# A two-layer graph network on one core: the whole program's instruction queues ordered by another model of durations

## The chip, the cores and the metric

One core of a Trainium2 chip. The metric is the device time of one execution in microseconds (us). The core has five engines with a queue of instructions each: TensorE (PE in the profile, with PEld for its weight loads), VectorE (DVE), ScalarE (ACT), GpSimd (POOL) and SyncE (SP), which here only starts transfers. A queue is fixed when the program is built.

## The reference

64 graphs of 256 nodes with 256 features each, in float32. Two layers, each followed by a residual sum and a layer norm.

```python
# layer 0, of one graph: adj and x are 256x256
deg = adj.sum(-1); deg = where(deg != 0, deg, 1); r = deg ** -0.5
h = (r[:, None] * adj * r[None, :] + max(alpha, 1e-10) * I) @ x
x = layernorm(x + h @ W.T + b)
# layer 1
xc = x.T
h = relu(bn1(conv1d(xc, conv1, width 1)))
x_conv = relu(bn2(conv1d(h, conv2, width 17, pad 8)) + xc).T
s = x @ w_se.T + b_se                      # 3 columns
A = exp(-squared_distance(s, s))           # 256x256
x_nmp = A @ relu(x @ w_msg.T + b_msg)
gi = concat(x_conv, x_nmp) @ w_ih.T + b_ih; gh = x @ w_hh.T + b_hh
r = sigmoid(gi_r + gh_r); z = sigmoid(gi_z + gh_z)
n = tanh(gi_n + r * gh_n)
x = layernorm(x + (1 - z) * n + z * x)
```

## The kernel before

Line numbers are those of the profile before.

**Rounds.** The 64 graphs go in four rounds of 16 (`Q = 16`, `NQ = 4`). The convolution of width 17 is done in the frequency domain: each graph gives 8 pieces of 32 nodes, so a round fills the 128 rows of a matmul with 16 x 8 pieces. A round has three stages.

1. *Graphs* (`graphs`, L879). For each graph `layer0` (L329) and `layer1` (L403) are generators that are stepped in turn. Layer 0: transposes of the adjacency (`p_adjT`, L361), a copy on ScalarE (L362), `p_hT` (L382), its copy (L387), `p_out` (L392), a sum on VectorE (L396), a layer norm. Layer 1: transposes of the result (`p_x1T`, L411) and their copy to `xn` (L412), the first convolution (`p_conv`, L420), its bias on VectorE (`h`, L423) and relu on ScalarE (L424), messages (`p_msg`, L441), the DFT (`p_dft`, L455) and its copy, transposed distance rows (`p_rows`, L468; `dist_l` L470 and `dist_r` L472), `p_dist` (L479), the exponential (L480) and mask (L481), and the sum over neighbours (`p_nmp`, L486).
2. *Products* (`products`, L528). In 12 steps the spectra are multiplied by the kernel's spectra `u`, which are streamed from memory (`p_k`, L510). `VM` is overwritten in place, and an inverse FFT (`real_transform`, `complex_begin`, `complex_end`) runs over it on VectorE, hundreds of operations of 0.4 to 0.7 us at L559 to L688. It ends with stores to `xc_d`.
3. *Gates* (`gru`, L766). For each graph: transposes of the convolution's result (`p_xcT`, L750), sums of inputs on GpSimd (`sums`, L761 to L764), seven blocks of `p_rz` (L780), their sums on VectorE (`first`, L793 and on), tanh on ScalarE, `p_n` (L817), `gn` (L822 to L826), a layer norm and the store. Each gate unit fills six PSUM tiles (four `p_rz`, two `p_n`), which take the four banks of the pool `psacc` in turn.

The stages of neighbouring rounds overlap: four gate units of a round run beside the next round's graphs, and the other twelve beside the next round's products. In round 0 there is other work beside the graphs: the 13 *weight sets* (`weights`, L274 to L296) that make `u`. A set loads 4 rows of taps, scales them (L279), does eight matmuls (`p_u`, L287), copies them to `u_set` (L290), forms a difference on VectorE (L292) and a sum on GpSimd (L293), and writes three arrays to `ud` (L295). `PLACES` (L877) says at which piece of a graph a piece of the other work is taken:

```python
PLACES = (("other",), ("layer0",), (), (), ("layer0",), ("other", "layer0"), ())
```

**What sets the order.** The generators set the order in which instructions are recorded, and with it their priority. Then a planner goes through the recorded program: it keeps a clock for each engine, advances it by a model of how long each instruction takes, and puts into each engine's queue, at each moment of that clock, the ready instruction of the highest priority. So a queue's order depends on the recorded order and on the modelled durations; an instruction that the model finds ready early can be queued ahead of others that were recorded before it. The chip keeps the queue's order whatever the real durations are. In three places an order is written by hand, with `tc.issue_after` (L219, L346, L372), all of them at the start.

**Buffers that bind.** PSUM: `ps` and `psacc` with four banks each. `taps`: 2. `u_set`: 2 for each of its four kinds. `xn`: 2. `sums`, `trz`, `nn`, `h`, `hT`, `msg`, `aT`: 1.

Of the kernel before, what the change touches and what calls it, by code (L numbers as in the profile page):

```python
# [26 lines left out]
def kernel(  # L27
# [39 lines left out]
    NQ = B // Q  # L67
    assert N == 256 and D == 256 and B % Q == 0 and TAPS == FL - NT + 1 and FL == 3 * NT // 2

    const = ctx.enter_context(tc.tile_pool(name="const", bufs=1))  # L70
    dram = ctx.enter_context(tc.tile_pool(name="dram", bufs=1, space=bass.MemoryType.DRAM))

# [986 lines left out]
```

## Time and profile before

| | us |
|---|---|
| device time, median of two runs | 2188.94 (2186.56 to 2191.32) |
| span of the profiled execution | 2186.0 |
| TensorE busy | 2067.5 (95%) |
| VectorE busy | 1547.1 (71%) |
| ScalarE busy | 831.2 (38%) |
| GpSimd busy | 664.5 (30%) |
| bytes moved | 305.64 MB, mean 140 GB/s |
| mean granted TensorE clock | 0.985 |

A float32 matmul stands in the profile as two records, so 4 matmuls are "x8". A record's own duration is longer than the distance to the next, since matmuls are pipelined: four matmuls of 256 columns start 1.73 us after the four before them. In a list of instructions the bracket says how long the engine sat idle before them and who released it. In the list of waits the numbers are the total, the number of times, and the longest. In time, the graphs of round 0 go to about 289 us; the products `p_k` of the four rounds lie at 289 to 393, 641 to 752, 1161 to 1271 and 1682 to 1790 us; what remains of a round's gates follows its products, then come the next round's graphs; after 1790 only gates are left.

### The profile page before, as it was taken

The numbers are of one execution on the slowest core, as the hardware profiler recorded it, in microseconds if no ns is written. First come the engines' busy times: TensorE is split into PE (matmuls) and PEld (weight loads), VectorE is DVE, ScalarE is ACT, GpSimd is POOL, SyncE is SP. The second block draws the span as 40 slices with busy tenths as digits, with TensorE's granted clock in tenths as the row PEclk, the third lists the DMA queues.
The fourth block names the chain that finished last, engine by engine and source line by source line (L and its number), as shares of the span: only waits on it lengthen the run. The fifth ranks groups of instructions, "written<-read, shape, count | busy, mean of one in ns | idle before, by whom it ended". The sixth has DMA issues, their size and how long they took to land.

```text
span 2186.0 us, 28897 instructions
## 1 busy us (share of the span) xinstructions
PE 2067.5 (95%) x9805; PEld 1750.7 (80%) x9805; DVE 1547.1 (71%) x3691; ACT 831.2 (38%) x1847; POOL 664.5 (30%) x640
## 2 busy tenths in 40 slices
PE   6999899969999988999999998899999999899998
PEld 5888778758888876888888887788888887778887
DVE  5555458875568799655557889855565879987766
ACT  3665533445531123455452122446543112222222
POOL 2445310122322233223231224322231223344442
PEclk9999999989999999999999999999999999999999
DMA  3765656443346644434336654433334654344441
GB/s 110 239 193 194 222 178 207 151 134 102 111 137 201 191 130 108 131 91 123 105 101 190 207 144 130 116 114 108 102 97 126 205 160 118 114 121 111 105 113 53
DMA packets 251331, 305.64 MB, mean 140 GB/s; under 512 B 18324, under 2 KB 229864, under 8 KB 251184
## 3 DMA queue, kind: packets, MB, share of 16 engines
q1 hardware_dynamic: 183680, 200.46, 30.0%
q10 hardware_dynamic: 44480, 67.39, 8.7%
q0 software_dynamic: 23024, 35.95, 8.2%
q8 instruction: 78, 1.28, 0.2%
q14 instruction: 69, 0.57, 0.1%
HBM read 200.62 MB, written 103.06 MB: 139 GB/s over the span
## 4 chain that ended last, share of the span: by engine, by line
PE 50%; DVE 14%; issue 6%; POOL 6%; ACT 4%; DMA 0%; ACTq 0%; POOLq 0%; SPq 0%; DVEq 0%
PE p_rz L780 18%; PE p_n L817 9%; PE p_k L510 8%; PE p_nmp L486 2%; PE p_out L392 2%; PE p_dft L455 2%; PE p_conv L420 2%; POOL sums L762 2%; PE p_hT L382 1%; PE p_msg L441 1%; POOL ln_rs L308 1%; POOL sums L764 1%; PE p_dist L479 1%; POOL sums L763 1%; DVE gn L822 1%
## 5 line engine op out<-in xcount | busy, mean ns | idle before, releaser
L780 PE MATMUL p_rz<-wrz,sums 128*128 128x256 f32 x1536 | 355.8, 383 | 19.4 <-DVE gn L822 9.8
L817 PE MATMUL p_n<-wn,inputs 128*128 128x256 f32 x1536 | 353.0, 383 | 16.2 <-DVE first L793 15.7
L780 PEld LDWEIGHTS p_rz<-wrz,sums 128*128 128x128 f32 x1536 | 288.4, 191 | 70.7 <-issue 15.8
L817 PEld LDWEIGHTS p_n<-wn,inputs 128*128 128x128 f32 x1536 | 286.6, 191 | 62.6 <-DVE first L793 19.0
L780 PE MATMUL p_rz<-wrz,inputs 128*128 128x256 f32 x1152 | 272.9, 380 | 2.4 <-ACT inputs L752 1.8
L308 POOL TENSOR_TENSOR ln_rs<-ln_rs,neg_half 128x2 f32<-128x2 f32 x129 | 100.2, 777 | 537.3 <-DVE ln_rs L307 451.5
L780 PEld LDWEIGHTS p_rz<-wrz,inputs 128*128 128x128 f32 x1152 | 216.7, 190 | 33.9 <-ACT inputs L752 3.8
L352 POOL TENSOR_TENSOR dis<-deg,neg_half 128x2 f32<-128x2 f32 x64 | 48.6, 760 | 425.1 <-DVE deg L350 320.4
L829 ACT ACTIVATE nn<-gn 128x256 f32<-128x256 f32 x128 | 53.2, 416 | 326.0 <-DVE gn L826 325.5
L510 PE MATMUL p_k<-u,VM 128*128 128x256 f32 x736 | 175.1, 380 | 0.0
L318 ACT ACTIVATE x_g<-x_g,ln_mr,ln_rs 128x256 f32<-128x256 f32 x128 | 70.0, 593 | 256.4 <-DVE ln_mr L316 256.4
L510 PEld LDWEIGHTS p_k<-u,VM 128*128 128x128 f32 x736 | 138.6, 190 | 19.6 <-DMA u<-ud 0.7
L455 PE MATMUL p_dft<-fwd,h 128*128 128x240 f32 x512 | 121.4, 382 | 24.2 <-ACT h L424 23.1
L761 POOL TENSOR_TENSOR sums<-inputs 128x384 f32<-128x384 f32 x64 | 69.6, 1087 | 230.2 <-issue 172.3
L420 PE MATMUL p_conv<-wc,xn 128*128 128x259 f32 x512 | 127.4, 391 | 12.1 <-ACT xn L412 12.1
L455 PEld LDWEIGHTS p_dft<-fwd,h 128*128 128x128 f32 x512 | 98.2, 196 | 41.2 <-ACT h L424 32.9
L382 PE MATMUL p_hT<-adjT,x 128*128 128x256 f32 x512 | 126.8, 392 | 2.2 <-ACT adjT L362 1.5
L486 PE MATMUL p_nmp<-aT,msg 128*128 128x256 f32 x512 | 123.6, 385 | 2.6 <-DVE aT L481 2.6
L375 POOL TENSOR_TENSOR x_t<-x_t,b_t 128x512 f32<-128x512 f32 x64 | 84.8, 1325 | 134.5 <-ACT x L374 94.0
L392 PE MATMUL p_out<-w,hT 128*128 128x256 f32 x512 | 122.8, 382 | 1.1 <-ACT hT L387 0.9
L441 PE MATMUL p_msg<-wmsg,xn 128*128 128x256 f32 x512 | 122.1, 381 | 0.0
L420 PEld LDWEIGHTS p_conv<-wc,xn 128*128 128x128 f32 x512 | 96.8, 192 | 31.5 <-ACT xn L412 17.3
(154 smaller groups left out, 3838.6 us busy)
## 6 DMA issues: line engine op xcount, KB each, us to landing
u<-ud SPq DMA_DIRECT2D x284, 256.0 KB
xn_d<-xn ACTq DMA_DIRECT2D x64, 512.0 KB
inputs<-xn_d SPq DMA_DIRECT2D x64, 512.0 KB
ud<-u_set POOLq DMA_DIRECT2D x39, 480.0 KB, 6.1
adj_t<-in_adj_dram SPq DMA_DIRECT2D x64, 256.0 KB
x_t<-in_x_dram SPq DMA_DIRECT2D x64, 256.0 KB
x_d<-x ACTq DMA_DIRECT2D x64, 256.0 KB
x_g<-x_d SPq DMA_DIRECT2D x64, 256.0 KB
```

The costliest lines, as they stand in the source:

```text
L308: nc.gpsimd.tensor_tensor(rs[:, : len(chunks)], rs[:, : len(chunks)], neg_half[:, : len(chunks)], op=ALU.pow)
L318: nc.scalar.activation(y[:, c, :], y[:, c, :], AF.Identity, bias=mr[:, c : c + 1], scale=rs[:, c : c + 1])
L375: nc.gpsimd.tensor_tensor(x_t, x_t, b0_t.unsqueeze(1).to_broadcast([P, NCH, D]), op=ALU.add)
L382: nc.tensor.matmul(p[:, k, :], x1[:, mc, k * P : (k + 1) * P], adjT[:, mc, 1 - mc : 3 - mc, :].rearrange("p n q -> p (n q)"), start=mc == ...
L392: nc.tensor.matmul(p[:, c, :], hT[:, k, c * P : (c + 1) * P], w0[:, k, :], start=k == 0, stop=k == DCH - 1)
L420: nc.tensor.matmul(p, x1T[:, k, c * P : (c + 1) * P], wc1[:, k, :], start=k == 0, stop=k == DCH - 1)
L441: nc.tensor.matmul(p[:, c, :], x1T[:, k, c * P : (c + 1) * P], wmsg[:, k, :], start=k == 0, stop=k == DCH - 1)
L455: nc.tensor.matmul(p[:, t0 * FL : t1 * FL], h[:, c, k * P : (k + 1) * P], fwd[:, first : first + t1 - t0, :].rearrange("p t f -> p (t f)") ...
L486: nc.tensor.matmul(p[:, k, :], msg[:, mc, k * P : (k + 1) * P], aT[:, mc].rearrange("p n q -> p (n q)"), start=mc == 0, stop=mc == NCH - 1,)
L510: nc.tensor.matmul(p[:, j * D : (j + 1) * D], v[:, k, :], u[:, k, :], start=k == 0, stop=k == DCH - 1)
L780: nc.tensor.matmul(p[:, j * D : (j + 1) * D], a[:, k], wrz[:, b, k], start=k == 0, stop=k == HALF - 1)
L817: nc.tensor.matmul(p[:, o * D : (o + 1) * D], lhsT, w, start=j == 0, stop=j == len(part) - 1)
```

## The change

One statement is added at the head of the kernel's function. It opens a block, held open to the end of the function, with an option that is off by default:

```diff
     assert N == 256 and D == 256 and B % Q == 0 and TAPS == FL - NT + 1 and FL == 3 * NT // 2
 
+
+    ctx.enter_context(tc.block(schedule_with_timeline_sim=True))
     const = ctx.enter_context(tc.tile_pool(name="const", bufs=1))
```

For all that is recorded in the block the planner keeps its clocks by the other model of durations it has, a timeline simulation of the instructions, in place of its usual one. The purpose is queues that fit durations nearer to the chip's. No operation, operand, buffer or transfer is added, removed or resized: all five engines get the same instructions, in another order. Line numbers after the change are two higher.

The two orders, built from the two sources, differ from the start on. Three excerpts of TensorE's queue, before and after, give the manner; the names are those of the tiles written, the numbers are matmuls:

```
graphs 0 and 1 of round 0, before: p_conv 4, p_u 4, p_adjT 4, p_msg 4, p_dft 4, p_rows 2, p_hT 4, p_dist 2, p_u 4, p_out 4, p_nmp 4, p_x1T 4, p_conv 1, p_u 4, p_conv 3
graphs 0 and 1 of round 0, after:  p_u 8, p_x1T 4, p_u 8, p_conv 4, p_adjT 4, p_msg 4, p_u 8, p_dft 4, p_rows 2, p_hT 4, p_u 8, p_dist 2, p_out 4, p_u 8, p_nmp 4, p_x1T 4, p_u 8, p_conv 4
graphs 5 to 15 of round 0, before: as above, p_u 8 in each up to graph 12
graphs 5 to 15 of round 0, after:  p_conv 4, p_adjT 4, p_msg 4, p_dft 4, p_rows 2, p_hT 4, p_dist 2, p_out 4, p_nmp 4, p_x1T 4
graphs beside gates, before: p_conv 4, p_adjT 4, p_msg 4, p_dft 4, p_rows 2, p_hT 4, p_dist 2, p_rz 6, p_xcT 4, p_out 4, p_nmp 4, p_x1T 4, p_n 6, p_conv 4
graphs beside gates, after:  p_conv 4, p_adjT 4, p_msg 4, p_rz 6, p_n 3, p_dft 4, p_rows 2, p_hT 4, p_n 8, p_dist 2, p_n 1, p_out 4, p_rz 7, p_nmp 4, p_x1T 4, p_conv 4
```

On VectorE the operations of the inverse FFT move against those of graphs and gates, and on GpSimd the sums and the writes of `ud` move against the layer norms.

## The prediction

> **What bounds the kernel now.** I read the page's first two parts, then the chain, then who TensorE waits for, then the worst stretch in order of time.
>
> ```profile
> PE 2067.5 (95%) x9805; PEld 1750.7 (80%) x9805; DVE 1547.1 (71%) x3691; ACT 831.2 (38%) x1847; POOL 664.5 (30%) x640
> PE   6999899969999988999999998899999999899998
> PE 50%; DVE 14%; issue 6%; POOL 6%; ACT 4%; DMA 0%; ACTq 0%; POOLq 0%; SPq 0%; DVEq 0%
> ```
>
> TensorE is busy in 95% of the span, so an order can win at most what it idles: 2186.0 - 2067.5 = 118.5 us, plus what a lowered clock stretched. The second row shows where: the start, slice 8 (the end of round 0) and small dips. The waits of TensorE itself (first rows of that view):
>
> ```profile
> PE p_dft L455 <- ACT h L424: 23.1, 9, 9.6
> PE p_n L817 <- DVE first L793: 15.7, 13, 2.4
> PE p_conv L420 <- ACT xn L412: 12.1, 11, 3.9
> PE p_rz L780 <- DVE gn L822: 9.8, 9, 1.6
> PE p_rz L780 <- POOL sums L762: 9.3, 8, 2.5
> PE p_dist L479 <- DVE dist_r L472: 7.5, 7, 1.4
> ```
>
> Each is a round trip through another engine with too little matmul work queued in between. The timeline of PE at the worst place shows two kinds:
>
> ```profile
> 447.87 2.02 PE L420 MATMUL p_conv<-wc,xn 128*128 128x259 f32 x8 [0.73 <-ACT xn L412]
> 449.73 0.60 PE L361 MATMUL p_adjT<-ident,adj_t 128*128 128x128 f32 x4
> 450.16 1.89 PE L441 MATMUL p_msg<-wmsg,xn 128*128 128x256 f32 x8
> 461.61 3.57 PE L455 MATMUL p_dft<-fwd,h 128*128 128x240 f32 x8 [9.56 <-ACT h L424]
> 470.44 0.69 PE L468 MATMUL p_rows<-ident,scols 128*128 128x128 f32 x2 [5.25 <-DVE scols L433]
> ```
>
> First, a convolution right behind the transposes p_x1T that feed it costs 0.73 us. Second, VectorE had FFT work queued ahead of h, and the DFT waited 9.56 us. The busy time by stretches gives the clock and the transfer rate:
>
> ```profile
> 60.00:90.00 30.00, 29.89 (x149) 24.82 (x149) 18.38 (x41) 17.08 (x40) 14.19 (x13) 1.00 0.79 248
> 452.00:475.00 23.00, 8.10 (x22) 5.59 (x22) 19.55 (x58) 7.19 (x11) 1.97 (x2) 0.63 0.40 133
> 1820.00:1960.00 140.00, 122.91 (x560) 101.88 (x559) 129.45 (x265) 32.31 (x66) 54.11 (x49) 1.00 0.42 118
> ```
>
> (Columns: stretch, length; busy PE, PEld, DVE, ACT, POOL; granted clock; DMA share; GB/s.) In the last stretch VectorE, 129.45 of 140 us, is the limit, not TensorE.
>
> **What the Trainium skill says.** "PSUM — Partial Sum Buffer", section Engine vs sequencer instructions: the queues of ScalarE, VectorE and GpSimd are strict FIFO, and matmuls start in program order. The trace agrees: the matmuls behind the DFT at 461.61 did not overtake it. So the queue order alone decides what a wait holds up. "TensorE: Matmul & The Clock Gate", section HAM oscillation, warns of idle gaps over some 3.4 us, after which the array runs at half clock. It agrees: behind the 9.56 us gap eight passes took 3.57 us instead of 1.89, at a mean clock of 0.63. "DMA: Bandwidth & Descriptors", section Specifications, gives about 358 GB/s of HBM per core. No stretch here reaches it; the busiest moved 248 at a share of 0.79, from which I estimate a ceiling of 248/0.79 = 314.
>
> **The change, part by part.** No instruction is added or removed: both programs have the same matmuls and vector instructions; only queue positions differ. I compared the two orders engine by engine and priced the work between marks with start-to-start times of the trace before (a 256-column matmul 0.43 us, a 128x512 VectorE operation 0.60, a 128x256 one 0.34). Line numbers are those before.
>
> 1. *Convolution behind its transposes (L411, L420).* A convolution waits for the copy of p_x1T for 0.73 us less the matmul time queued between. Before, 9 of 64 graphs have less than that: 6.0 us in sum. After, 39 have, 34 of them nothing at all: 25.6 us. TensorE is the bound there and nothing hides it: **+19.6 us**.
> 2. *The other round trips.* The same count for rows to dist (0.92 us needed), dist to nmp (1.7) and hT to out (0.9) gives 0.9, 3.3 and 0.3 us before, 3.7, 5.1 and 0.9 after: **+5 us**. Between convolution and DFT neither order has less than 1.7 us, which the trace shows to be enough when VectorE is free.
> 3. *The weight sets (L287 to L295).* Before, eight p_u matmuls sit in each of 13 graphs, spread over 203 us of TensorE work. After, there are four sets to a graph and all 13 within 81 us (graph to graph 26.4, 26.4, 23.0 us of TensorE work, then twelve graphs of about 12.6 with none). VectorE (52 us of work in that stretch) and GpSimd (64 us) fit. Transfers do not: 39 writes of ud x 0.49 MB = 19.2 MB, taps 4.2, gate weights 2.4, and x, adj, xn and x1 of three to four graphs 4.7, sum 30.5 MB; without the last two sets' writes, which may land later, 27.6 MB. At my 314 GB/s that is 88 us, at the observed 248 it is 111. Each u_set has two buffers, held from the copy (3.5 us for eight matmuls) over sums (3.0) and issue (1.2) to landing (6.1 median): 14 us for two sets, or 7 us each, against 26.4/4 = 6.6 us of TensorE work. So the stall is 7 to 30 us; I take **+20 us**, and 0 to 45 for the range. What waits behind it: the copy on ScalarE for a free u_set holds the copies of the graph queued behind, and then TensorE.
> 4. *Start.* After, the first p_u stand before p_x1T of graph 0, and dft_w before ln_mr on VectorE. Before, TensorE did p_x1T and two convolutions (2.2 us) before it waited for dft_w until 36.26; after, it sits idle from about 28 to 36, over the clock gate's limit. 2.2 us plus some 4 us of slow clock: **+6 us**.
> 5. *VectorE at the end of round 0.* Before, the stretch between two graphs' h (L423) that overloads VectorE is one of 23.0 us of its work against 12.6 us of TensorE's, and in all 12 us more than TensorE has. After, three in a row, 20.7, 22.2 and 15.8 against 12.6: 21 us more. **+9 us**.
> 6. *VectorE at the tails of rounds 1 to 3.* From one gate unit (gru) to the next, marked by first (L793): before, 13.6 to 17.1 us of VectorE against 14.8 to 16.6 of TensorE in the worst units, overload 2 to 3 us a round. After, units of 21.5 and 19.8 against 14.8 and 14.3 in rounds 1 and 2, and 20.2, 20.1, 18.4 against 14.8 in round 3: overload 12, 12 and 14 us. But the totals over the tail are equal (round 3: 127 and 128 us), and at parity before already lost some 17 us in 1820 to 1960. What is paid in a lump after is then not paid in small change. I take **+4 us a round, +12**; the bounds are 0 and 32.
> 7. *An early GpSimd sum.* Before, sums (L761) stood ahead of ln_rs at 265 us and waited for its input's transfer; TensorE lost 5.1, 0.9 and 1.7 us and ran at half clock (0.64 from 265 to 284). Worth about 14 us in all. After, a sum is again placed ahead of layer norms, among graphs 5 to 6, but transfers are lighter there. I take half: **-7 us**.
>
> Scalar copies, loads of adj and x, stores: nothing, since they lie beside TensorE. Sum: 19.6 + 5 + 20 + 6 + 9 + 12 - 7 = 65 us. 2188.9 + 65 = **2254 us**.
>
> **Rivals.**
> *A, nearly no change.* The transfers keep up, since the first bits of a set can run ahead, and the tails even out: parts 1, 2 and half of 4 stay and the 14 us of part 7 come back: 20 + 5 + 3 - 14 = +14, 2203 us. For it: in the stretch 60 to 90 the DMA share was only 0.79. Against: 27.6 MB in 81 us would need 341 GB/s.
> *B, faster.* The new order dissolves the waits at 452, 787 to 865, 1306 to 1385 and 1820 to 1960 (about 22, 14, 15 and 17 us, with some 18 us of slow clock) and the sum at 265 (14), at the price of part 1 and 2 alone: 25 - 100 = -75, 2114; with half of them, 2164. For it: a model that knows durations better would place VectorE's FFT work better. Against: the queue of VectorE shows the overload grown, not shrunk.
> *C, much slower.* Full bounds: 45 for part 3, 32 for part 6, and slow clock on top of part 5 (10): +65 + 25 + 20 + 10 = +120, 2309 us. For it: every gap over 3.4 us is paid twice.
>
> **How the numbers follow.** Forecast 2254 (2225 to 2290): 0.50. A: 0.25. B: 0.09. C: 0.16. The 2% bounds are 2145 and 2233. B lies mostly below or near 2145: faster 0.07. A, the rest of B and a little of the forecast lie within: 0.31. Slower: 0.62. The range takes the forecast, most of A and up to C: 2188 to 2310.
>
> **What would show it.** Step 1: the wait of p_conv for xn grows from 12 to some 30 us. Step 3: in 35 to 140 us, TensorE clearly under its work and DMA share above 0.85, u_set waiting for ud. Step 4: a gap of some 8 us before the first p_u. Step 5: three gaps of 3 to 9 us at p_dft between 370 and 460 us. Step 6: gaps at p_n or p_rz that come in two or three clusters, not one per unit. If TensorE's idle time is below 118 us, the forecast is wrong; if it is much above and sits elsewhere, its reasons are.

## The result, and the profile after

The changed kernel takes 2299.25 us (2296.28 to 2302.22) against 2188.94: a ratio of 1.051, 95% interval 1.0475 to 1.0538, so 110 us slower. The prediction had the direction and the range, but 65 us of the 110.

The page of the changed kernel (line numbers are two higher than before), busy time and TensorE's slices:

```profile
PE 2115.1 (92%) x9805; PEld 1787.5 (78%) x9805; DVE 1562.7 (68%) x3691; ACT 834.0 (36%) x1847; POOL 674.5 (29%) x640
...
PE   7889999789999987998999997998999997899998
```

The instruction counts are those of before. The profiled span grew by 108.5 us (2186.0 to 2294.5), and these rows split it in two: TensorE idles 179.4 us in place of 118.5 (+60.9), and the same 9805 matmuls are busy 47.6 us longer. The second part is the clock: the records show half clock for 172.8 us in place of 65.5. Of TensorE's busy time 143.8 us fall into these periods, before 41.7. At half speed, half of the difference is excess: by this estimate 51 us, near the 47.6. The dips now come in every round.

What TensorE waits for (us in total, times, longest):

```profile
PE p_conv L422 <- ACT xn L414: 36.7, 39, 3.6
PE p_n L819 <- DVE trz L796: 24.4, 5, 5.6
PE p_n L819 <- DVE gn L824: 14.9, 5, 5.2
PE p_n L819 <- DVE first L795: 10.0, 8, 2.5
PE p_out L394 <- ACT hT L389: 9.3, 4, 2.9
...
PE p_dft L457 <- ACT h L426: 7.7, 5, 3.1
```

Two things replaced p_dft's 23.1 us. p_conv waits for its own transposes' copy 39 times, and p_n waits for gate results of VectorE, seldom but for up to 5.6 us. Busy time by stretches (stretch, length; busy PE, PEld, DVE, ACT, POOL; clock; DMA share; GB/s) shows the two bad kinds of place, the crowded weight sets and a tail:

```profile
35.00:140.00 105.00, 88.59 (x342) 70.11 (x342) 57.42 (x80) 44.42 (x91) 55.06 (x52) 0.83 0.82 244
820.00:910.00 90.00, 68.63 (x279) 56.60 (x279) 88.08 (x201) 14.52 (x31) 36.92 (x23) 0.91 0.35 100
```

In the first, no unit is full: TensorE loses 16 us to gaps and about as much to a clock of 0.83 (an estimate: half of the 33.8 us of matmul time that fell to half clock). In the second, VectorE hardly pauses and TensorE starves. The timeline of VectorE there, then of TensorE, shows how:

```profile
896.05 0.42 DVE L828 SCALAR_TENSOR_TENSOR gn<-gn 128x256 f32<-128x256 f32 x1
896.38 0.68 DVE L795 TENSOR_TENSOR first<-p_rz,brz_t 128x512 f32<-128x512 f32 x1
896.98 4.74 DVE L690 SCALAR_TENSOR_TENSOR VM<-turn,VM 128x256 f32<-128x256 f32 x6
901.64 0.68 DVE L843 SCALAR_TENSOR_TENSOR nn<-trz,nn 128x512 f32<-128x512 f32 x1
902.25 0.75 DVE L592 SCALAR_TENSOR_TENSOR turn<-VM 128x256 f32<-128x256 f32 x2
902.92 0.68 DVE L844 TENSOR_TENSOR x_g<-x_g,nn 128x512 f32<-128x512 f32 x1
903.52 0.68 DVE L796 TENSOR_TENSOR trz<-first,p_rz 128x512 f32<-128x512 f32 x1
```

```profile
904.25 4.54 PE L819 MATMUL p_n<-wn,inputs 128*128 128x256 f32 x12 [4.14 <-DVE trz L796]
```

Between first and trz, which follow each other in the text of a gate unit, stand eight FFT operations and two other gate operations. p_n needs the accumulator that trz frees, waits 4.14 us, and then its six matmuls (x12) take 4.54 us; the six before them, unslowed, took 2.75. Here is VectorE's queue over one gate unit (G is first, g another gate operation, F the FFT, n layer norm), from 807.5 us before and from 874.4 us after:

```
GnnngnFngnFFFFgFgFFFgFFFFgFgFgFFgFgFgFg
GFFgFFFFFFgFFFgggFFFnngFnngFFFngFFgFgnFgggFFFFFFg
```

The longest run of FFT operations grew from four to six.

### The profile page after: what moved, and what is told of

It is laid out like the page before. It is cut to its first block, busy times and chain, and to the rows that moved or that the text cites. A ratio compares the mean times of both kernels' runs of the same rounds, so it can differ in the third digit from the quotient of the medians.

```text
span 2294.5 us, 28979 instructions
## 1 busy us (share of the span) xinstructions
PE 2115.1 (92%) x9805; PEld 1787.5 (78%) x9805; DVE 1562.7 (68%) x3691; ACT 834.0 (36%) x1847; POOL 674.5 (29%) x640
## 3 DMA queue, kind: packets, MB, share of 16 engines
q1 hardware_dynamic: 183680, 200.46, 28.6%
## 5 line engine op out<-in xcount | busy, mean ns | idle before, releaser
L819 PE MATMUL p_n<-wn,inputs 128*128 128x256 f32 x1536 | 373.1, 396 | 49.3 <-DVE trz L796 24.4
L819 PEld LDWEIGHTS p_n<-wn,inputs 128*128 128x128 f32 x1536 | 300.1, 199 | 102.6 <-DVE trz L796 26.7
L782 PE MATMUL p_rz<-wrz,sums 128*128 128x256 f32 x1536 | 357.7, 380 | 1.6 <-DVE gn L824 1.4
L782 PE MATMUL p_rz<-wrz,inputs 128*128 128x256 f32 x1152 | 282.2, 381 | 4.1 <-DVE trz L796 4.1
L310 POOL TENSOR_TENSOR ln_rs<-ln_rs,neg_half 128x2 f32<-128x2 f32 x129 | 120.9, 972 | 424.3 <-DVE ln_rs L309 398.7
L422 PE MATMUL p_conv<-wc,xn 128*128 128x259 f32 x512 | 135.6, 409 | 36.7 <-ACT xn L414 36.7
L763 POOL TENSOR_TENSOR sums<-inputs 128x384 f32<-128x384 f32 x64 | 88.9, 1388 | 273.4 <-issue 208.0
L394 PE MATMUL p_out<-w,hT 128*128 128x256 f32 x512 | 133.1, 405 | 18.3 <-ACT hT L389 9.3
L488 PE MATMUL p_nmp<-aT,msg 128*128 128x256 f32 x512 | 128.7, 397 | 5.9 <-DVE aT L483 5.9
L394 PEld LDWEIGHTS p_out<-w,hT 128*128 128x128 f32 x512 | 99.0, 200 | 43.3 <-ACT hT L389 20.0
L741 POOL DMA_DIRECT2D xc_g<-x_d x64 | 78.4, 1260 | 157.3 <-DMA xc_g<-xc_d 80.7
```

The lines of the kernel that those rows point to most:

```text
L310: nc.gpsimd.tensor_tensor(rs[:, : len(chunks)], rs[:, : len(chunks)], neg_half[:, : len(chunks)], op=ALU.pow)
L394: nc.tensor.matmul(p[:, c, :], hT[:, k, c * P : (c + 1) * P], w0[:, k, :], start=k == 0, stop=k == DCH - 1)
L422: nc.tensor.matmul(p, x1T[:, k, c * P : (c + 1) * P], wc1[:, k, :], start=k == 0, stop=k == DCH - 1)
L488: nc.tensor.matmul(p[:, k, :], msg[:, mc, k * P : (k + 1) * P], aT[:, mc].rearrange("p n q -> p (n q)"), start=mc == 0, stop=mc == NCH - 1,)
L741: nc.gpsimd.dma_start(CONV[g], x1_d[g // Q][g % Q].rearrange("(c p) d -> p c d", p=P), accum_op=ALU.add)
L763: nc.gpsimd.tensor_tensor(S[:, 2], A11, A21, op=ALU.subtract)
```

## The experiments

Each run was timed together with the kernel before. The table has, from the traces, the length of the stretches between the first p_real of each round, the first product of its products stage (us). A trace shows one execution, which can lie some way from the median of its run (sets_spread 5 us, fft_spread 6, before_filled 9, conv_filled 13), so differences of columns and of medians do not agree to the microsecond.

| stretch | before | after | cut_none | cut_first | cut_rest | sets_spread | fft_spread | two_undone |
|---|---|---|---|---|---|---|---|---|
| start to round 0 | 288.9 | 320.5 | 288.5 | 325.5 | 287.9 | 293.8 | 320.3 | 289.1 |
| to round 1 | 352.5 | 366.6 | 352.3 | 354.1 | 357.7 | 369.7 | 369.0 | 368.4 |
| to round 2 | 519.5 | 545.4 | 519.4 | 519.4 | 549.3 | 545.8 | 531.3 | 532.6 |
| to round 3 | 519.5 | 546.5 | 517.8 | 517.9 | 543.5 | 543.5 | 529.0 | 528.7 |
| to the end | 505.6 | 515.5 | 505.9 | 505.7 | 517.4 | 516.8 | 525.2 | 517.7 |

**Where it is lost: the model in one part alone.** A plain block without the option leaves the order of every engine as before: what counts is the model alone. Two blocks let the model be chosen by part (F1, F2: with the option or not):

```diff
+    first_part.enter_context(tc.block(F1))
     xin, ain = {}, {}
...
+    first_part.close()
+    ctx.enter_context(tc.block(F2))
     ustream = ctx.enter_context(tc.tile_pool(name="ustream", bufs=6))
```

> The program is cut in two blocks of its own, setup with round 0's graphs and everything behind it, with neither on the other model; three pairs of loads move behind the cut. Queues are almost the same as before, so this is the base for the two runs that switch the model in one part. All theories: 2189 to 2200 us, ratio 1.000 to 1.005.

> As cut_none, with the other model in the first part alone (setup and round 0's graphs). The changed kernel's first p_real came 31.6 us later than before. Theory (the losses of the parts are independent and add up): 30 to 35 us over cut_none, ratio about 1.014 to 1.018. Rival (late weights or other left-overs of the first part disturb the rounds behind it): 45 us or more over cut_none. Rival (an early part that ends later is made up later by work that was waiting on nothing else): under 15 us.

> As cut_none, with the other model in the second part alone (all four rounds). The prediction put about 9 us at the end of round 0, 4 us at each of three tails and some 12 us on graphs' round trips here, less 7 us: about 30 us over cut_none. The trace of the changed kernel puts 77 us here (14 in round 0's tail, 26 and 27 up to the weights' products of rounds 2 and 3, 10 behind the last). Theory (independent parts): 70 to 80 us over cut_none, and cut_first and cut_rest together make 100 to 115.

Measured: cut_none 2187.38 (ratio 0.9998, 0.9988 to 1.0009); cut_first 2227.14 (1.0172, 1.0157 to 1.0187), 40 us over cut_none; cut_rest 2258.99 (1.032, 1.0303 to 1.0337), 72 us. They add up to 111, the whole change. cut_first is 5 us beyond its 30 to 35, 37 us of it before the first p_real. The model's loss in the first part stays there, and two thirds of the loss lie in the rounds, where the prediction had about 30 us.

**The weight sets.** In taps3 the tile "taps" has bufs=3 in place of 2. In sets_spread a p_u group is queued behind the last p_x1T transpose or p_dist matmul traced so far:

```diff
+                with tc.issue_after(BEHIND[0]):
                     for h in range(2):
                         nc.tensor.matmul(p[:m, h], DFT_W[0][:, i]..., tp[:, j + h], ...)
```

> The changed kernel with three buffers in place of two for the loaded tap sets; TensorE's queue stays the same but for two matmuls. Theory (trace: the gaps of 3.4 to 3.8 us ahead of p_u wait for a set's taps, and each is followed by some 10 us at half clock): the gaps ahead of p_u shrink, first p_real 10 to 20 us earlier, total 2280 to 2290. Rival, as in the prediction's step 3 (buffers of u_set and the write-out of ud hold the crowded sets back): no change within 4 us. Rival (the loads themselves, at DMA's rate): the waits move from one set to another, within 5 us.

> The changed kernel with each half of a weight set queued on TensorE no earlier than the piece of the graph behind which the text puts it: 8 p_u matmuls between two graphs again, as before, in place of 32. Theory (crowding the sets costs what the first part lost, less its round trips): first p_real at 295 to 303 us in place of 320.5, total 2274 to 2282. Rival (the graphs' bare round trips, which stay, are the larger part): first p_real at 312 or later, total 2290 or more.

taps3: 2288.96 (1.0457, 1.0425 to 1.0489), whose interval still touches that of the changed kernel; in its own stretch the first p_real came 8.1 us earlier (312.4), just under what I expected. sets_spread: 2266.19 (1.0354, 1.0327 to 1.0381), 33 us less by the medians, and by the traces 26.7 less before the first p_real: more than expected. Crowding is most of the first part's loss of 31.6. What late taps do is seen in the timeline of the changed kernel, in the same eight matmuls (x16) with and without a gap ahead:

```profile
100.47 3.62 PE L289 MATMUL p_u<-taps,dft_w 85*120 85x256 f32 x16
...
109.62 6.93 PE L289 MATMUL p_u<-taps,dft_w 85*120 85x256 f32 x16 [3.37 <-DMA taps<-in_conv2T_dram]
...
132.83 6.26 PE L289 MATMUL p_u<-taps,dft_w 85*120 85x256 f32 x16 [3.53 <-DMA taps<-in_conv2T_dram]
```

A late set costs some 3.4 us of waiting and 2.6 to 3.3 us in slow matmuls. With three buffers two such gaps are left, at early sets (6.18 and 3.84 us), and one p_conv now waits 5.05 us for xn. That is some 8 of the 27 us; the rest of the crowding was not taken apart.

**The round trip at p_conv.** p_adjT moves up in the text, and p_conv is queued behind it; the same edit in the kernel before is before_filled.

```diff
-    PLACES = (("other",), ("layer0",), (), (), ("layer0",), ("other", "layer0"), ())
+    PLACES = (("other", "layer0"), (), (), (), ("layer0",), ("other", "layer0"), ())
...
+            with tc.issue_after(ADJ_LAST[0]):
                 for k in range(DCH):
                     nc.tensor.matmul(p, x1T[:, k, c * P : (c + 1) * P], wc1[:, k, :], ...)
```

> The changed kernel with the four transposes of p_adjT queued between p_x1T and p_conv: 8 graphs of 64 are left with nothing between, as before, in place of 34. Theory (prediction's step 1): TensorE's wait of p_conv for xn falls from 36.7 us to 12 to 16, nothing takes its place: total 2274 to 2283 with some half clock saved. Rival (p_adjT is then missing somewhere else, ahead of p_hT or p_msg): waits move to these, total 2290 or more.

> The kernel before, with the four transposes of p_adjT between p_x1T and p_conv where nothing was: 2 graphs with nothing between in place of 8. Theory (a bare round trip costs its 0.7 us and more): p_conv's wait falls from 12.1 us to 4 to 6, total 2180 to 2186. Rival (the few bare ones sit where TensorE waits for VectorE anyway): within 3 us of 2187.6.

conv_filled: 2280.55 (1.043, 1.04 to 1.046), 19 us less, though p_conv's wait only fell to 26.1 us (35 times) and not to 12 to 16: the total fits the theory, its reason only in part. The transposes are too short: 8 graphs have nothing between, as meant, but elsewhere the four transposes fill 0.44 us of a round trip of 0.73, and most of the waits left are the 0.29 between the two. What else gave the 19 us is not accounted for; p_n's wait for gn fell as well, from 14.9 to 4.6 us. before_filled: 2240.17 (1.0243, 1.0214 to 1.0272), 52 us slower, where neither theory had it more than 3 us slower. Its waits show a rival that I had not named:

```profile
PE p_dft L457 <- ACT h L426: 60.4, 32, 18.5
...
PE p_conv L422 <- ACT xn L413: 7.6, 7, 3.5
```

p_conv's wait fell from 12.1 to 7.6 us, and p_dft's rose from 23.1 to 60.4. In part that is the filler, for the transposes had been work between p_conv and p_dft: 28 of the 32 waits, of 0.2 to 2.2 us, make 26 us (before seven such, 8 us). The other part is VectorE's queue, which the edit moved too. Four of p_dft's waits are of 4.5 to 18.5 us, far more than four transposes could cover; in the longest, nearly 11 us of VectorE's work, almost all of it the transform, stand between the two halves of h. And p_nmp waits 3.15 us for aT five times (18.2 us in all, before 2.6), because a scaling of taps whose load was late stands ahead of aT:

```profile
495.16 0.42 DVE L425 TENSOR_TENSOR h<-p_conv,bc 128x259 f32<-128x259 f32 x1
...
506.34 0.41 DVE L425 TENSOR_TENSOR h<-p_conv,bc 128x259 f32<-128x259 f32 x1
```

```profile
106.05 2.52 DVE L279 TENSOR_TENSOR taps<-taps,scale 85x1024 f32<-85x1024 f32 x1 [3.67 <-DMA taps<-in_conv2T_dram]
108.49 0.68 DVE L483 TENSOR_TENSOR aT<-aT,adjT 128x512 f32<-128x512 f32 x1
```

So an order edit on TensorE changed two queues, and how much of the 52 us the missing filler costs alone is not shown.

**VectorE in the tails.** The inverse transform's second half is held behind the last gate operation on VectorE traced so far:

```diff
+    def behind_gates(stage):
+        while True:
+            with tc.issue_after(GATED[0]) if GATED else ExitStack():
+                if next(stage, "end") == "end":
+                    return
+            yield
...
-        end = complex_end(q)
+        end = behind_gates(complex_end(q))
```

> The changed kernel with the vector work of the inverse transform's second half queued no earlier than the gate work that stands before it in the text: the long runs of transform work between two gate operations are thinned out, and some moves to the graphs behind. Theory (prediction's step 6 with a larger size): the p_n waits for gn, first and trz fall by half, and the stretches from the weights' last product to graph 38's and 54's p_conv shrink from 247 us to about 235 each: total 2270 to 2282. Rival (VectorE has the same sum to do and only shifts the wait, to the graphs behind or to the transformed rows that the next gates read): within 8 us of 2299.

2270.16 (1.037, 1.0337 to 1.0403), 29 us less. The stretch from the weights' last product of round 1 to graph 38's p_conv, first in the changed kernel, then here (columns as above):

```profile
805.60:1052.70 247.10, 219.12 (x1003) 184.88 (x1001) 186.26 (x446) 88.03 (x193) 78.79 (x67) 0.96 0.36 105
```

```profile
808.40:1040.20 231.80, 217.78 (x1002) 184.42 (x1000) 187.78 (x445) 87.40 (x191) 73.00 (x67) 0.96 0.37 111
```

The same matmuls, the same VectorE work, 15.3 us less time; 15.0 in round 2. Before needs 232.5 there. Over the whole execution p_n's waits for first, trz and gn fell from 49.3 to 9.7 us, while those of p_dft and p_rows rose from 15.3 to 32.8. So it is not how much VectorE has to do but what stands ahead of a gate operation. In the last round the hold did harm, as this line of the timeline shows, and the stretch to the end grew by 9.7 us:

```profile
2029.05 1.12 PE L760 MATMUL p_xcT<-ident,xc_g 128*128 128x128 f32 x4 [18.72 <-DMA xc_g<-x_d]
```

**Together.** two_undone has the edits of sets_spread and of fft_spread, the latter without the last round; three_undone also that of conv_filled.

> The changed kernel with the weight sets spread and, in rounds 1 and 2 alone, the transform behind the gate work (not in the last round, where fft_spread's p_xcT waited 18.7 us for transformed rows). Theory (the two losses lie in different stages and add up): 33 us and two tails of 15 us off, total 2232 to 2242; the last stage, from the last product of round 3 to the end, stays at 400 us in place of fft_spread's 408. Rival (the later transform only pays where the first part is late): 2250 or more.

> As two_undone, with p_adjT's transposes between p_x1T and p_conv as well. conv_filled took 18.7 us off, 8.7 of them before the first p_real, where the spread sets may have taken them already. Theory: 8 to 14 us below two_undone, 2220 to 2232. Rival (as the kernel before_filled showed, the transposes are then missing ahead of p_dft): p_dft's wait for h grows to 40 us or more and the total is the same as two_undone's or longer.

two_undone: 2233.43 (1.0217, 1.0203 to 1.0231), 66 us less than the changed kernel; the two losses add up. The first part is back at 289.1 us. three_undone: 2228.37 (1.0193, 1.0177 to 1.0208), 5 us less, below the 8 to 14 expected and with overlapping intervals; p_dft's wait rose from 30.0 to 39.6 us while p_conv's fell from 27.3 to 21.4, an exchange between the two round trips, here without long waits (p_dft's longest is 3.7 us).

**A better kernel than before?** Graph 22's work, where the kernel before waits 9.56 and 5.25 us, was put ahead of the transform, with `with tc.high_priority(offset=200)` around the operations on h and the score columns (h_first) or around all of layer1 for that graph (graph_first).

> The kernel before, with the vector and scalar work on graph 22's h and score columns put ahead of the inverse transform's; TensorE's queue stays as it is and 11 VectorE instructions move. In the trace of before TensorE waits there 9.6 us (p_dft for h) and 5.2 us (p_rows for the columns), and 17 us at half clock follow. Theory (the two waits are queue order alone): 6 to 14 us off, 2174 to 2182. Rival (the transform has to be done before V may be overwritten, and TensorE only waits two groups later for a bank): within 3 us of 2188.

> As h_first, with all pieces of graph 22 put ahead. Theory: also takes the waits behind p_rows, 10 to 18 us off before, 2170 to 2178. Rival: the transform ends that much later, the copies into V with it, 2185 or more.

h_first: 2191.32 (1.0025, 1.0014 to 1.0035); graph_first: 2195.52 (1.0045, 1.0031 to 1.0059). Both are slower, on the rivals' side (h_first 0.3 us beyond its rival's 3). The two gaps of 9.6 and 5.2 us went, and one of h_first took their place:

```profile
470.80 3.46 PE L383 MATMUL p_hT<-adjT,x 128*128 128x256 f32 x8 [16.64 <-DVE adjT L365]
```

In graph_first p_hT waits 17.68 us in the same place. adjT belongs to another graph's layer 0, and neither run put it ahead; whether VectorE must finish the transform there in any order was therefore not tried. The wait was moved, not removed. No version tried beats the kernel before.

## Why the prediction was right in direction and short by 45 us

- **Step 1 (+19.6).** Right in the trace: 34 graphs have nothing between p_x1T and p_conv, as counted, and p_conv's wait grew by 24.6 us, the predicted sign. Its worth depends on the rest: 19 us alone, about 5 once sets and tails are undone.
- **Step 2 (+5).** p_out's waits for hT (now 9.3 us) and p_nmp's (2.6 to 5.9) grew, p_dist's did not (7.5 to 5.8). Not run alone.
- **Step 3 (+20, 0 to 45) and step 4 (+6).** Together 26 forecast; spreading the sets gives 26.7 before the first p_real. The size held, the reasons less, so it held by some luck. I named ud's writes and u_set's buffers; the DMA share over 35 to 140 us is 0.82, not above 0.85, and no copy into u_set waits for ud in the trace. What waits is VectorE's scaling of the taps for their loads (33.9 us in 9 waits, before none), and three tap buffers alone give 8 us. Step 4's gap of 8 us is 2.7, but half clock in the first 50 us is 20.5 us in place of 6.8.
- **Step 5 (+9).** The stretch to round 1 is 14.1 us longer. Of the sign, one half: between 414 and 506 us p_dft waits three times, up to 3.1 us, and p_rows three times likewise. Not run alone.
- **Step 6 (+4 a round).** This is the term that failed most. The lump is there and grew by about what I had: over the three worst gate units of round 1, first to first, VectorE is busy 67.5 us and TensorE 51.8 (before 60.7 and 54.6), 15.6 us over against 6.1, where I had 12 against 2 to 3. What failed is its price: I argued that equal totals of VectorE work make up for most of a lump. fft_spread shows equal totals and 15 us a round: 30 for rounds 1 and 2 against 8. The predicted sign, clusters at p_n, is there. Round 3's share was not undone; its last stretch is 9.9 us longer, so that with it the bound of 32 for the three rounds may have been too low.
- **Step 7 (-7).** p_rz's wait for sums fell from 9.3 to 0.3 us.
- **The clock.** I counted 4 us, at the start only, and left it to rival C elsewhere; busy TensorE time grew by 47.6. It is not a separate cause: it follows the gaps, and undoing two of the causes returned 28.6 of it (2115.1 to 2086.5).

Open: the 47 us by which two_undone is still over before. By the table they lie in all four later stretches, 9 to 16 us each. p_conv, p_dft and p_rows, and p_n's waits for trz in round 3 (16.0 us in the changed kernel), are what TensorE waits for there, but they were not undone one by one. Each of the edits also lets the planner move other work, as before_filled shows, so a saving belongs to the edit as a whole. Why this model's durations lead to this order was not tried either.

## What to carry to other kernels

Price a queue order by what stands between one operation and the next on the same chain, not by an engine's sums: 446 VectorE operations of 186 us cost 15 us more or less by their place alone. Before filling a bare round trip, ask which other one the filler covers now and whether the filler is long enough, and compare the queues of all engines after the edit, not only the one edited. And count a price for the clock beside TensorE's gaps: 60.9 us more of them brought 47.6 us of slower matmuls in the changed kernel, though 47.5 us more brought 13.7 in before_filled.

## What the runs showed of the hardware

- **Gaps under 3.4 us can slow the clock.** In the changed kernel a gap of 2.1 us at 854.8 us, with no other in the 12 us before, is followed by half clock at 857.4 for 3.4 us. In all 14 traces together I took the gaps that stand alone (at full clock, with no other gap over 0.3 us in the 12 us before or the 3.5 us behind). Half clock began during or up to 3.5 us behind 24 of the 34 gaps of 2 to 3 us and 26 of the 27 over 3 us, but only 2 of the 25 of 1.6 to 2 us and none of the 127 of 1 to 1.6 us. (Many are the same place of the program in another run, and the lengths rest on modelled ends of matmuls.) In the changed kernel the periods are of 3.4, 6.8, 10.2 and 20.5 us, apart from the last. The Trainium skill, "TensorE: Matmul & The Clock Gate", section HAM oscillation, warns of gaps over some 3.4 us; here shorter ones did it too, and the measurement decides.
- **VectorE against GpSimd.** The operation at L690, with both inputs in SBUF, took at most 0.42 us in the 67 cases of the changed kernel in which no GpSimd operation ran beside it, and 0.66 us in the mean, up to 1.22, in the 61 in which one did. At L425, where an input comes from PSUM, 75 operations beside GpSimd took at most 0.43 us. The six at 896.98 took 4.74 us while GpSimd ran four sums from 896.4 to 900.8 us. "SBUF — State Buffer" of the Trainium skill, section SBUF: two separate sides, says that a VectorE operation with two SBUF inputs and a GpSimd operation that reads SBUF exclude each other. The trace agrees. It is not what the change costs, though: in the stretch to graph 38 the time that such operations took beyond their usual is by my estimate some 22 us both before and after.
